# Keys and queries: one store of parts per pair of blocks, replicated when loaded; stores of values and late weights issued by ScalarE's queue

## The chip, the cores and the metric

The kernel runs on one core of a Trainium2 chip. The metric is the device time of one execution in microseconds (us); the slowest core counts, and here there is only one. The engines are called as the profile calls them: PE (matrix multiply, with PEld for its weight loads), DVE, ACT, POOL, and SP, which only issues transfers (DMAs). A transfer is issued by the queue of SP or of ACT, and 16 DMA engines move its bytes.

## The reference, cut to what matters

The input `x` is four images of 64 x 64 pixels with 256 channels, float32. Layer 0 is full self-attention over the 4,096 pixels of each image:

```
q, k, v = x@Wq + bq, x@Wk + bk, x@Wv + bv        # q and k have 32 channels, v has 256
x = gamma * softmax(q @ k^T) @ v + x
```

Layer 1 works on the result: a 3x3 depthwise convolution (three outputs per channel), two 1x1 convolutions with a GELU between them and a residual, then attention over the 3x3 neighbourhood of each pixel, and a second residual. The change touches layer 0 alone: how q, k and v get from where they are computed to where attention reads them.

## The kernel before, in words

Everything is in channels-first layout. An image is cut into 8 blocks of 512 pixels (`NB`). A **slot** is one block of queries: 4 images x 8 blocks = 32 slots. In each slot the kernel goes through the 8 groups `G` of 512 keys of its image, so one group is: four energy matmuls (`energy`, L334, tile `e`), two exponentials on ACT (`weight`, L342, tile `p`), and eight products with the values (`product`, L353, tile `acc`), one half of the exponentials at a time. Energies of group G+1 are issued ahead of the products of group G. `e` has one buffer, so the energies of a group wait until both exponentials of the group before have read it. `p` has three buffers, `ka` (keys of a group) and `v` (values of a group) have three each, `qa` (queries of a slot) has two.

To get q*k in float32 accuracy from a faster matmul format, each of q and k is split into a high part `st` (rounded) and a low part `sl` (what is missing). `project_qk(s)` computes q and k of the two blocks s and s+1 at once (one PSUM tile of 128 rows: q of s, k of s, q of s+1, k of s+1, 32 rows each), ACT writes the high part (L251) and an unrounded copy (L252), DVE subtracts (L253). `st` and `sl` have one buffer each, so the next pair waits for every transfer that reads this one. A key tile `ka` then holds 4 x 32 rows: high, high, low, low; a query tile `qa` holds high, low, high, low. One 128-row matmul thus sums all four products of parts.

Before the change this replication is made on the way out: for each pair of blocks SP issues sixteen 64 KB stores to DRAM (L268 for keys to `packed_k`, L274 for queries to `packed_q`), each of 32 rows, and a group's keys come back in one 256 KB load of 128 rows (`load_keys`, L284), a slot's queries likewise (`spread_queries`, L321). The exception is the first pair: the first queries and the first group's keys go straight from `st`/`sl` into `qa`/`ka`, four copies on SP (L262) and four on ACT (L259).

`project_v` computes 256 pixels of values; ACT copies them out of PSUM (L309) and SP stores them to `packed_v` (L310). For the first image they also stay in `v`; all other values are loaded from `packed_v` (`load_values`, L288).

The order on each engine is the order of the program text (`manual_schedule`). Ahead of slot 0 stand: blocks 0 and 1 fetched, `project_qk(0)`, values of blocks 0 and 1, `project_qk(2)`, `load_keys(0, 1)`, the energies of group 0, the values of block 2. In slot 0, after the second half of group 0, stand `early(4)` (fetch of blocks 4 and 5 from DRAM, L234, tile `xc`, then `project_qk(4)`) and half of the values of block 3; after that of group 1 the other half and `early(6)`; after those of groups 2 to 5 the values of blocks 4 to 7. In the middle of slot 0 (`point == NG`, group 4) SP loads the weights of layer 1 (L80 through `loaded`, and L1228), between the two exponentials of group 5. In the last slot of each image but the last (7, 15, 23), the projections of the next image stand between the groups. Layer 1 starts with slots 2 and 3, at a lag.

Waits are on semaphores. The framework gives the completion of each transfer to one of eight semaphores in turn, across both queues, and a transfer also waits for the one that had its semaphore before it, if nothing later has waited for that.

Of the kernel before, what the change touches and what calls it, by code (L numbers as in the profile page):

```python
# [9 lines left out]
F32 = mybir.dt.float32  # L10
# [6 lines left out]
P = 128  # L17
B, H, W, C = 4, 64, 64, 256
N = H * W
CQK = C // 8  # L20
CH = C // P
HP, WP = H + 2, W + 2
NB = 512
# [15 lines left out]
GRP = P // CQK  # L39
# [3 lines left out]
NSLOT = B * NBLK  # L43
# [10 lines left out]
def attention_then_perception_kernel(  # L54
# [19 lines left out]
    nc = tc.nc  # L74
# [3 lines left out]
    def loaded(src, name, shape=None, queue=None):  # L78
        t = const.tile(list(shape or src.shape), F32, tag=name, name=name)
        (queue or nc.sync).dma_start(out=t, in_=src)  # L80
        return t
# [10 lines left out]
    def unshifted():  # L92
# [6 lines left out]
        def tile_of(shape, tag, name, bufs=1):  # L99
            return pool.tile(shape, F32, tag=tag, name=name, bufs=bufs)  # L100
# [37 lines left out]
        for r in range(4):  # L138
            nc.scalar.dma_start(
                out=bqk2[r * CQK : (r + 1) * CQK, :], in_=b_qk[:, r % 2 : r % 2 + 1]  # L140
# [17 lines left out]
        for r in range(KR):  # L158
            m = near[r * KW : (r + 1) * KW]
            for half in range(2):  # L160

                for sign in (1, -1):
                    nc.gpsimd.affine_select(
                        out=m[:, half], in_=m[:, half], compare_op=ALU.is_ge, fill=0.0,
# [13 lines left out]
        for q in range(0, P, SQ):  # L178
            part = fold[q : q + SQ].rearrange("p (j r) -> p j r", r=SQ)
            nc.gpsimd.affine_select(  # L180
                out=part, in_=part, compare_op=ALU.not_equal, fill=1.0,
# [18 lines left out]
        queries, keys, values, staged = {}, {}, {}, {}  # L200

        packed_q, packed_k = (tc.dram_tile([P, B * N], F32, name=n) for n in ("packed_q", "packed_k"))
        packed_v = tc.dram_tile([P, NSLOT * TPB * C], F32, name="packed_v")
        Q_PARTS, K_PARTS = (0, 1, 0, 1), (0, 0, 1, 1)

        def rows_of(j):
            return slice(j * CQK, (j + 1) * CQK)

        def fetch(s):

# [27 lines left out]
        def project_qk(s):  # L240

            ps = bank("m", f"qk_{s}")
            for kin in range(CH):
                for r in range(2):
                    nc.tensor.matmul(
                        ps[2 * r * CQK : 2 * (r + 1) * CQK, :],
                        lhsT=wqk[:, kin].rearrange("p s d -> p (s d)"),
                        rhs=staged[s + r][:, kin, :], start=(kin == 0), stop=(kin == CH - 1),
                    )
            high, low = (tile_of([P, NB], tag, f"{tag}_{s}") for tag in ("st", "sl"))  # L250
            nc.scalar.activation(high.bitcast(F32R), ps, AF.Identity, bias=bqk2)  # L251
            nc.scalar.activation(low, ps, AF.Identity, bias=bqk2)  # L252
            nc.vector.tensor_tensor(low, low, high, ALU.subtract)  # L253
            parts = (high, low)
            if s == 0:
                queries[0] = tile_of([P, NB], "qa", "qa_0", 2)
                keys[0, 0] = tile_of([P, NB], "ka", "ka_0_0", 3)
                for j in range(GRP):
                    nc.scalar.dma_start(  # L259
                        out=keys[0, 0][rows_of(j), :], in_=parts[K_PARTS[j]][CQK : 2 * CQK, :]  # L260
                    )
                    nc.sync.dma_start(  # L262
                        out=queries[0][rows_of(j), :], in_=parts[Q_PARTS[j]][:CQK, :]
                    )
            for r in range(2):
                at = 2 * r * CQK
                for j in range(GRP):
                    nc.sync.dma_start(  # L268
                        out=packed_k[rows_of(j), bass.ts(s + r, NB)],
                        in_=parts[K_PARTS[j]][at + CQK : at + 2 * CQK, :],  # L270
                    )
                if s + r:
                    for j in range(GRP):
                        nc.sync.dma_start(  # L274
                            out=packed_q[rows_of(j), bass.ts(s + r, NB)],
                            in_=parts[Q_PARTS[j]][at : at + CQK, :],
                        )

        def block(s, G):
            return s - s % NBLK + G  # L280

        def load_keys(s, G):
            keys[s, G] = tile_of([P, NB], "ka", f"ka_{s}_{G}", 3)
            nc.sync.dma_start(out=keys[s, G], in_=packed_k[:, bass.ts(block(s, G), NB)])  # L284

        def load_values(s, G):
            values[s, G] = tile_of([P, TPB, C], "v", f"v_{s}_{G}", 3)
# [5 lines left out]
        def project_v(s, pair, tag="m"):  # L293
            xc = staged[s]
            if s >= NBLK:
                v = tile_of([P, 2, C], "vs", f"vs_{s}_{pair}", 2)
            else:
                if pair == 0:
                    values[0, s] = tile_of([P, TPB, C], "v", f"v_0_{s}", 3)
                v = values[0, s][:, 2 * pair : 2 * pair + 2, :]  # L300
            ps = bank(tag, f"v_{s}_{pair}")
            for i in range(2):
                for kin in range(CH):
                    nc.tensor.matmul(  # L304
                        ps[:, i * C : (i + 1) * C],
                        lhsT=xc[:, kin, bass.ts(2 * pair + i, P)], rhs=wv[:, kin, :],
                        start=(kin == 0), stop=(kin == CH - 1),
                    )
            nc.scalar.copy(v, ps.rearrange("p (t c) -> p t c", c=C))  # L309
            nc.sync.dma_start(  # L310
                out=packed_v[:, bass.ts(2 * s + pair, 2 * C)], in_=v.rearrange("p t c -> p (t c)")
            )

# [4 lines left out]
        def spread_queries(s):  # L318

            queries[s] = tile_of([P, NB], "qa", f"qa_{s}", 2)  # L320
            nc.sync.dma_start(out=queries[s], in_=packed_q[:, bass.ts(s, NB)])  # L321


        energies, weights, sums, accs, lsums, lrdens = {}, {}, {}, {}, {}, {}
# [772 lines left out]
        for i in range(2):  # L1097
            project_v(1, i)
        project_qk(2)
        load_keys(0, 1)  # L1100
        energy(0, 0)
        weight(0, 0, 0)
        weight(0, 0, 1)
# [6 lines left out]
        wlv = pool.tile([P, CH, C], F32, tag="wlv", name="wlv")  # L1110
# [11 lines left out]
        for slot in range(NSLOT):  # L1122
# [3 lines left out]
            k, a = slot - LAG_HID, slot - LAG_ATT  # L1126
# [50 lines left out]
            for point in range(points):  # L1177
                G, half = divmod(point, 2)
                after = slot + (G + 1) // NG, (G + 1) % NG
                if half == 0:  # L1180
                    ahead = slot + (G + 2) // NG, (G + 2) % NG
                    if ahead[0] < NSLOT:
                        load_keys(*ahead)
                    if 0 < ahead[0] < NSLOT:
                        load_values(*ahead)
                    if G == NG // 2 and slot + 1 < NSLOT:
                        spread_queries(slot + 1)
                    if after[0] < NSLOT:
                        energy(*after)
                if after[0] < NSLOT:  # L1190
                    weight(*after, half)
                for do in jobs[point]:
                    do()
                product(slot, G, half)

                if point == 0:
                    add_up(slot, 0, 0)
                if point < points - 1:
                    add_up(slot, *divmod(point + 1, 2))
                else:  # L1200
                    partial_sums(slot)


                if slot < NSLOT - 1:
                    to = sum(share[: point + 1])
                else:
                    to = min(n_steps, -(-(point + 1) * n_steps // (points - 2)))
                    if point < 3:
                        to = min(to, n_mixed // MULT)
                while stepped < to:  # L1210
                    next(conv, None)
                    stepped += 1
                if slot == 0 and point == NG:

                    next(combine)
                    blqk = loaded(b_lqk, "blqk")
                    wperc = loaded(w_perc, "wperc")
                    bperc = loaded(b_perc, "bperc")
                    wup1 = loaded(w_up1, "wup1")
                    bup1 = loaded(b_up1, "bup1")  # L1220
                    wup2 = loaded(w_up2, "wup2")
                    mix_weights(
                        *blocks_of(wup1, MULT, C), *(wmix[:, i] for i in range(4))
                    )
                    y = blocks_of(wup2, CH, P)
                    mix_weights(*y, wmix2[:, 0], wmix2[:, 1], y[1], wmix2[:, 2])
                    bup2 = loaded(b_up2, "bup2")
                    nc.sync.dma_start(out=wlv, in_=w_qkv[:, :, 2 * C :])  # L1228
                    blv = loaded(b_lv.partition_broadcast(P), "blv", [P, C])
                if nxt and half == 1:  # L1230
                    for do in nxt[G]:
                        do()
                    if slot and G + 2 < NBLK:
                        fetch(slot + 1 + G + 2)
# [470 lines left out]
```

## Time and profile before

| what | value |
|---|---|
| time, median of 3 runs | 3399.32 us (3399.2 to 3399.37) |
| the profiled execution | 3399.62 us, its span 3397.9 us |
| PE busy | 3367.3 us (99% of the span) |
| DVE, ACT, POOL busy | 2746.6, 1071.8, 347.5 us |
| DMA | 293.33 MB, mean 86 GB/s |
| loads of keys (L284) | 255 of 256 KB, median 4.0 us to landing |
| loads of values (L288) | 248 of 512 KB, median 3.7 us |
| stores of keys and queries (L268, L274) | 252 of 64 KB, median 1.7 us |
| stores of values (L310) | 64 of 256 KB, median 2.0 and 2.2 us |

The span is the time between the first and the last instruction of the profiled execution; 1.7 us lie around it. A row of the profile's instruction groups gives an engine's busy time for one line of the code, the mean length of one instruction, and the idle time before it with what ended it. The chain of waits goes back from the last instruction to what released each step. The table of windows gives, for a stretch of time, the busy time of each engine, the clock that PE was granted (1.00 is full), the share of time in which the 16 DMA engines were busy (1.00 is all of them), and the rate of all transfers. A transfer's line has the time that its queue took to issue it; when it has landed stands in the list of transfers.

### The profile page before, as it was taken

The numbers are of one execution on the slowest core, as the hardware profiler recorded it, in microseconds if no ns is written. First come the engines' busy times: TensorE is split into PE (matmuls) and PEld (weight loads), VectorE is DVE, ScalarE is ACT, GpSimd is POOL, SyncE is SP. The second block draws the span as 40 slices with busy tenths as digits, with TensorE's granted clock in tenths as the row PEclk, the third lists the DMA queues.
The fourth block names the chain that finished last, engine by engine and source line by source line (L and its number), as shares of the span: only waits on it lengthen the run. The fifth ranks groups of instructions, "written<-read, shape, count | busy, mean of one in ns | idle before, by whom it ended". The sixth has DMA issues, their size and how long they took to land.

```text
span 3397.9 us, 32797 instructions
## 1 busy us (share of the span) xinstructions
PE 3367.3 (99%) x11678; PEld 2117.9 (62%) x11678; DVE 2746.6 (81%) x4455; ACT 1071.8 (32%) x1344; POOL 347.5 (10%) x541
## 2 busy tenths in 40 slices
PE   8999999999999999999999999999999999999999
PEld 4556666666666666666666666666666666666655
DVE  1388888877889888876888898887688888988895
ACT  2233333333333333332333323333233333233331
POOL 1100011100111100110011111001110111110031
PEclk8999999999999999999999999999999999999999
DMA  5432222353222222235222222223522222222200
GB/s 153 137 103 69 75 69 77 94 160 100 78 66 86 86 65 81 72 103 151 94 81 78 66 82 89 65 81 112 161 74 73 81 77 67 82 89 65 70 13 26
DMA packets 178091, 293.33 MB, mean 86 GB/s; under 512 B 75008, under 2 KB 76288, under 8 KB 177792
## 3 DMA queue, kind: packets, MB, share of 16 engines
q1 hardware_dynamic: 177248, 290.56, 27.6%
q8 instruction: 95, 1.56, 0.2%
q10 hardware_dynamic: 672, 0.59, 0.1%
q14 instruction: 76, 0.62, 0.1%
HBM read 240.49 MB, written 50.07 MB: 86 GB/s over the span
## 4 chain that ended last, share of the span: by engine, by line
PE 92%; DVE 6%; SPq 1%; DMA 1%; issue 0%; ACT 0%; ACTq 0%; POOL 0%; DVEq 0%; POOLq 0%
PE acc L353 48%; PE e L334 7%; PE hid_de L611 5%; PE hid_gf L611 5%; PE hid_bc L611 5%; PE lv L924 3%; DVE perc L506 3%; PE lo L1058 3%; PE v L304 3%; PE hid_a L611 2%; PE s L965 2%; PE dx_cd L563 1%; PE dx_ab L563 1%; PE dx_eg L563 1%; DVE den L367 1%; PE g_cd L563 1%
## 5 line engine op out<-in xcount | busy, mean ns | idle before, releaser
L353 PE MATMUL acc<-p,v 128*128 128x512 f32 x4096 | 1833.4, 593 | 0.5 <-DVE o L418 0.5
L353 PEld LDWEIGHTS acc<-p,v 128*128 128x128 f32 x4096 | 770.4, 190 | 794.7 <-issue 775.4
L506 DVE SCALAR_TENSOR_TENSOR perc<-xp,wperc,perc 128x512 f32<-128x512 f32 (+2 forms) x1554 | 1107.4, 774 | 27.4 <-ACT perc L502 27.3
L342 ACT ACTIVATE p<-e 128x1024 f32<-128x1024 f32 x512 | 523.9, 1024 | 1673.6 <-PE e L334 745.9
L367 DVE TENSOR_TENSOR den<-den,p 128x1024 f32<-128x1024 f32 x480 | 585.9, 1221 | 67.9 <-ACT p L342 66.2
L334 PE MATMUL e<-qa,ka 128*128 128x512 f32 x1024 | 365.0, 478 | 11.0 <-DMA ka<-packed_k 11.0
L990 POOL TENSOR_TENSOR lp<-lp,near 128x396 f32<-128x396 f32 x60 | 89.7, 1494 | 2426.1 <-ACT lp L985 2426.1
L334 PEld LDWEIGHTS e<-qa,ka 128*128 128x128 f32 x1024 | 190.4, 190 | 141.2 <-issue 107.7
L611 PE MATMUL hid_de<-perc,wmix 128*128 128x256 f32 x720 | 165.2, 379 | 0.0
L611 PEld LDWEIGHTS hid_de<-perc,wmix 128*128 128x128 f32 x720 | 136.8, 190 | 43.7 <-issue 21.5
L512 DVE TENSOR_TENSOR perc<-perc 128x256 f32<-128x256 f32 x360 | 150.4, 432 | 8.2
L634 ACT ACTIVATE hid<-hid,bup 128x512 f32<-128x512 f32 x120 | 80.1, 714 | 219.7 <-DVE hid L618 219.7
L502 ACT ACTIVATE perc<-xp,bperc,wperc 128x512 f32<-128x512 f32 x192 | 145.3, 805 | 1.7 <-DVE xp L424 1.7
L1013 POOL TENSOR_TENSOR lsum<-lsum,lp 128x99 f32<-128x99 f32 (+1 forms) x179 | 123.1, 694 | 11.7
L924 PE MATMUL lv<-wlv,h 128*128 128x256 f32 x520 | 122.4, 379 | 0.0
L304 PE MATMUL v<-wv,xc 128*128 128x256 f32 x512 | 116.6, 380 | 1.5 <-ACT sl L252 1.4
L1058 PEld LDWEIGHTS lo<-lp,lv 128*128 128x128 f32 x732 | 104.9, 191 | 17.5 <-issue 9.8
L304 PEld LDWEIGHTS v<-wv,xc 128*128 128x128 f32 x512 | 96.9, 190 | 29.3 <-issue 15.0
L924 PEld LDWEIGHTS lv<-wlv,h 128*128 128x128 f32 x520 | 98.7, 190 | 15.5 <-issue 2.2
L1058 PE MATMUL lo<-lp,lv 128*128 128x99 f32 (+1 forms) x732 | 104.7, 291 | 0.0
L342 ACT ACT_TABLE_LOAD x60 | 77.0, 1283 | 82.0 <-PE e L334 81.9
L618 DVE TENSOR_TENSOR hid<-hid_bc,hid 128x512 f32<-128x512 f32 x60 | 41.5, 691 | 73.5 <-PE hid_bc L611 73.5
(198 smaller groups left out, 3125.6 us busy)
## 6 DMA issues: line engine op xcount, KB each, us to landing
v<-packed_v SPq DMA_DIRECT2D x248, 512.0 KB, 3.7
ka<-packed_k SPq DMA_DIRECT2D x255, 256.0 KB, 4.0
xp<-in_x SPq DMA_DIRECT2D x30, 528.0 KB, 4.6
xc<-in_x SPq DMA_DIRECT2D x56, 256.0 KB, 3.9
out<-lo SPq DMA_DIRECT2D x56, 256.0 KB, 2.0
packed_v<-vs SPq DMA_DIRECT2D x48, 256.0 KB, 2.0
qa<-packed_q SPq DMA_DIRECT2D x31, 256.0 KB, 4.0
packed_v<-v SPq DMA_DIRECT2D x16, 256.0 KB, 2.2
```

What stands on the lines that cost most here:

```text
L304: nc.tensor.matmul(ps[:, i * C : (i + 1) * C], lhsT=xc[:, kin, bass.ts(2 * pair + i, P)], rhs=wv[:, kin, :], start=(kin == 0), stop=(kin = ...
L334: nc.tensor.matmul(e[:, j, :], lhsT=key[:, bass.ts(j, P)].bitcast(F32R), rhs=queries[s].bitcast(F32R), start=True, stop=True,)
L342: nc.scalar.activation(p, energies[s, G][:, 2 * half : 2 * half + 2, :], AF.Exp)
L353: nc.tensor.matmul(accs[s][c], lhsT=v[:, 2 * half + i, bass.ts(c, P)], rhs=p[:, i, :], start=(first and i == 0), stop=(G == NG - 1 and hal ...
L367: nc.vector.tensor_tensor(den, den, p, ALU.add)
L502: nc.scalar.activation(acc, win, AF.Identity, bias=bperc[:, half, j : j + 1], scale=wt)
L506: nc.vector.scalar_tensor_tensor(acc, win, wt, acc, ALU.mult, ALU.add)
L512: nc.vector.tensor_tensor(t[:, to, :], t[:, a, :], t[:, b, :], op)
L563: nc.tensor.matmul(ps[:, n * C : (n + 1) * C], lhsT=w(j), rhs=values(j), start=(j == 0), stop=(j == kin - 1),)
L611: nc.tensor.matmul(ps[:, n * C : (n + 1) * C], lhsT=w(j), rhs=mixes[s, j][:, kind, :], start=(j == 0), stop=(j == MULT - 1),)
L924: nc.tensor.matmul(ps[:, half * C : (half + 1) * C], lhsT=keys_of(s, t, half, kin), rhs=wlv[:, kin, :], start=(kin == 0), stop=(kin == CH ...
L1058: nc.tensor.matmul(pv[:, rows, columns(half)], lhsT=lvs[block, t, half][:, bass.ts(c, P)], rhs=near_ws[block, half][:, t, of, :], start=(i ...
```

## The change

- `packed_q` and `packed_k` are replaced by one array `packed`, which holds, for each pair of blocks, high and low parts of q and k once each. `st` and `sl` become one tile `both` (still one buffer), and SP issues one 512 KB store per pair (L269 of the kernel after).
- `load_parts` (its transfers are at L212) makes the replication on loading, in two transfers of 64 rows each. For keys, each transfer reads 32 rows twice (`to_broadcast([2, ...])`); for queries, each reads the high and the low rows. `load_keys` and `spread_queries` use it.
- For the first pair, the queries and the keys of groups 0 and 1 are copied straight from the tile (twelve copies, all on SP, L268), and `load_keys(0, 1)` is gone.
- The stores of values (L304) and the late weights of layer 1 are issued by ACT's queue instead of SP's.

```diff
-        packed_q, packed_k = (tc.dram_tile([P, B * N], F32, name=n) for n in ("packed_q", "packed_k"))
+        packed = tc.dram_tile([NSLOT // 2, 2, 2, 2, CQK, NB], F32, name="packed")
...
+        def load_parts(to, s, which):
+            pair, r = divmod(s, 2)
+            part = packed[pair, :, r, which]
+            for i in range(2):
+                of = part[i : i + 1].to_broadcast([2, CQK, NB]) if which else part
+                nc.sync.dma_start(out=to[2 * i * CQK : 2 * (i + 1) * CQK, :], in_=of)
...
-            high, low = (tile_of([P, NB], tag, f"{tag}_{s}") for tag in ("st", "sl"))
+            both = tile_of([P, 2, NB], "st", f"st_{s}")
+            high, low = both[:, 0, :], both[:, 1, :]
...
             if s == 0:
                 queries[0] = tile_of([P, NB], "qa", "qa_0", 2)
...
-            for r in range(2):
-                at = 2 * r * CQK
-                for j in range(GRP):
-                    nc.sync.dma_start(
-                        out=packed_k[rows_of(j), bass.ts(s + r, NB)],
...
+                for G in range(2):
+                    keys[0, G] = tile_of([P, NB], "ka", f"ka_0_{G}", 3)
+                for part, G in ((0, 0), (1, 0), (0, 1), (1, 1)):
+                    for i in range(2):
+                        for to, at, from_ in (
+                            (queries[0], 2 * i + part, 0), (keys[0, G], 2 * part + i, 2 * G + 1)
+                        )[G:]:
+                            rows, of = (slice(j * CQK, (j + 1) * CQK) for j in (at, from_))
+                            nc.sync.dma_start(out=to[rows, :], in_=both[of, part, :])
+            nc.sync.dma_start(
+                out=packed[s // 2].rearrange("a r q d n -> (r q d) a n"), in_=both
+            )
...
-            nc.sync.dma_start(out=keys[s, G], in_=packed_k[:, bass.ts(block(s, G), NB)])
+            load_parts(keys[s, G], block(s, G), 1)
...
             nc.scalar.copy(v, ps.rearrange("p (t c) -> p t c", c=C))
-            nc.sync.dma_start(
+            nc.scalar.dma_start(
...
-            nc.sync.dma_start(out=queries[s], in_=packed_q[:, bass.ts(s, NB)])
+            load_parts(queries[s], s, 0)
...
         project_qk(2)
-        load_keys(0, 1)
         energy(0, 0)
...
-                    wup1 = loaded(w_up1, "wup1")
+                    wup1 = loaded(w_up1, "wup1", queue=nc.scalar)
...
-                    nc.sync.dma_start(out=wlv, in_=w_qkv[:, :, 2 * C :])
-                    blv = loaded(b_lv.partition_broadcast(P), "blv", [P, C])
+                    nc.scalar.dma_start(out=wlv, in_=w_qkv[:, :, 2 * C :])
+                    blv = loaded(b_lv.partition_broadcast(P), "blv", [P, C], queue=nc.scalar)
```

## The prediction

> **What bounds the kernel now.** First the engines' busy time and the totals of waits, to see whose time is the kernel's.
>
> ```profile
> PE 3367.3 (99%) x11678; PEld 2117.9 (62%) x11678; DVE 2746.6 (81%) x4455; ACT 1071.8 (32%) x1344; POOL 347.5 (10%) x541
> ```
>
> PE is idle for 3397.9 - 3367.3 = 30.6 us. Its own waits name what the change is about:
>
> ```profile
> PE e L334 <- DMA ka<-packed_k: 11.0, 4, 8.4
> PE qk L245 <- DMA xc<-in_x: 5.1, 2, 4.7
> ```
>
> (Total us, times, longest.) Both long waits are in slot 0, as the chain of waits for the first 160 us shows (start, length, what):
>
> ```profile
> 28.17 0.43 SPq L274
> 28.59 0.04 issue
> 28.64 3.16 DMA ka<-packed_k
> 31.80 0.14 issue
> 31.93 2.05 PE e L334 x4
> ...
> 57.36 4.73 DMA xc<-in_x
> 62.09 0.04 issue
> 62.13 3.67 PE qk L245 x6
> 65.81 1.45 PE e L334 x4
> ...
> 77.58 0.92 PE e L334 x4
> ...
> 100.06 0.92 PE e L334 x4
> ```
>
> The first `ka` load stands behind sixteen stores on SP (22.19 to 28.59); the second `xc` fetch stands behind sixteen more and a store of values that waits for ACT. The last three e rows are the energies of groups 3, 4 and 6 of slot 0, 11.24 us apart per group. From 65.81 the chain is PE without a gap to the end of slot 0. The windows view adds the clock (us, then PE, PEld, DVE, ACT, POOL busy, clock, DMA share, GB/s):
>
> ```profile
> 60.00:80.00 20.00, 19.62 (x52) 9.55 (x52) 4.63 (x5) 5.51 (x7) 0.00 (x0) 0.84 0.47 116
> 190.00:252.00 62.00, 62.00 (x181) 32.15 (x180) 60.01 (x90) 19.56 (x21) 3.89 (x5) 1.00 0.31 98
> ```
>
> In slot 2 (second row) PE never waits: what happens to PE in slot 0 reaches the end, unless a transfer comes late.
>
> **What the Trainium skill says.** "DMA: Bandwidth & Descriptors", section "Why a DMA increments its semaphore by 16 and not by 1": a transfer from SP or ACT runs on the largest k up to 16 that divides the outermost dimension (not 1) of both its source and its destination, on the lowest-numbered k engines. In the trace of before the single packets are recorded: 16,736 packets of 4 bytes = 16 x 1,046 transfers, so all ran on 16; none had a small outermost dimension. The new loads have one. In the built program a key load's source is 2 x 32 x 512 (the 2 with stride 0), a query load's 2 x 32 x 512; the destination has 64 rows. So **k = 2**: engines 0 and 1 carry all keys and queries. No run so far shows it. Same page, "Queues, rings and completion order": on each engine one queue's descriptors are consumed in order, and queues alternate; the trace agrees, `v` (3.7 us to land) and the `ka` issued 0.4 us after it (4.0) finish one behind the other. "TensorE: Matmul & The Clock Gate", Part 1: after an idle window PE restarts at half clock; the 0.84 after the wait at 57 to 62 agrees.
>
> **The price of a load on two engines.** 256 KB are 128 packets of 2,048 bytes, 64 on each engine. Packet records: median 84 ns, so 64 x 84 = 5.4 us; 0.7 on 16 engines. The window of slot 2 gives 98/(0.31 x 16) = 19.8 GB/s for an engine, so 6.6 us; the page's Specifications give 27 GiB/s, so 4.5. I take 5.4, the record of just this packet in the quiet slot 2; ends 4.5 and 6.6. The first packet starts 2.4 us after issue (a load of slot 1 issued at 136.6); I take 0.6 from the last one to landing.
>
> **Startup, edit by edit.** Twelve copies on SP from 10.33 at 0.5 each (rows of L262: 0.43 to 0.6) end at 16.4. ACT no longer issues copies (four, 0.7 each), but four stores of values (0.45 to 0.55); before the second `st` it has time for that. One 512 KB store follows; from 64 KB in 1.7 and 256 KB in 2.2 us I get 2.8, landing at 19.2. `st` of pair 1, which waits for it, starts at 19.2 (before 20.18). Two ACT passes (1.27) and two exponentials (1.94) later, 22.5, the energies of group 1 can start: keys lie ready. Gain 31.93 - 22.5 = 9.4.
>
> PE then has 2.05 + 7.82 and wants `xc` of block 4 at 32.4. SP: store of pair 1 at 21.3, landed 24.1, two key issues (0.45 each) to 25.0. Engines 0 and 1 carry them from 26.5 to 31.9; the four `xc` transfers' shares stand behind, to 34.5, landed 35. The projection ends at 36 instead of 34.3. With 1.93 of values, energies of group 2 at 37.9 (45.59). Then 0.93 + 6.87 + 1.74: second `xc` wanted at 47.5. Store at 38.4, keys on engines 0 and 1 41.4 to 46.8, `xc` landed 49.8, projection ends 50.4. **Energies of group 3: 50.5 against 65.81, gain 15.3.** The 1.5 us by which SP waited for values is gone in it.
>
> **The wait that comes.** Store of pair 3 at 52.6. From 55.8 engines 0 and 1 have without pause: keys of groups 4, 5, 6, queries of slot 1 (4 x 5.4 = 21.5), two further loads (1.6), keys of group 7 and of the next slot's group 0 (10.8); and from ACT's queue four stores of values (8 packets each, 2.7), `wup1` (8 x 0.467 = 3.7) and `wup2` (1.3). Sum 41.6: done at 97.4, landed 98.0. ACT needs this: in the built program its nine late weights wait, by the eight semaphores in turn, for earlier transfers; `wlv` for the second half of the next slot's first keys. They stand between the exponentials of group 5. So `wlv` issues at 98.0, `blv` at 98.5, the exponential runs 99.0 to 100.0, and energies of group 6, behind it, start at 101 with queueing. PE's own work would have been ready at 50.5 + 3 x 11.24 = 84.2. **Group 6: 101 against 100.06, +0.9: the gain is used up.** PE idled 16 us and restarts cold: +2.7 (after the wait at 62 before: 3.67 for six of eight projections that take 1.94 in all, and 1.45 for energies of 0.92).
>
> **Slots 1 and 2.** A group is 7.8 us of PE. Engines 0 and 1: keys 5.4, values 1.75 (the window's 0.31 x 7.8 = 2.42 us less 0.67 for keys), queries 5.4/8: 7.8. Just saturated; keys have 15 us from issue to use, so they slip through with +2 (bounds 0 and 5). From slot 3 on a group takes over 10 us.
>
> **Costed at nothing.** 48 later stores of values on ACT (0.45 each): ACT sits idle 3.5 us before such an exponential (679.7 us in 194 waits for products); without that cover, +21.6. Extra SP issues (285 second halves): SP mostly waits. DMA bytes on the way out halve: nothing waits for them later.
>
> **Sum**, against the profiled 3399.62 (0.3 above the median): 0.9 + 2.7 + 2 = +5.6, so **3405**, at the slow edge of no change. A measurement here tells 0.2% (6.8 us) from nothing. The ends of the two-engine price: at 4.5 (70 ns a packet) the 384 packets of keys and queries before group 6 take 5.4 less, the two `xc` waits 1.8, slots 1 and 2 lose nothing: 3396; at 6.6 (103 ns) +7.3 + 2.4 + 13: 3428, which is rival 2 at its worst. With 2 us for startup either way the main case's own range is 3396 to 3412.
>
> **Rivals.**
> (1) Transfers run on 16 engines all the same. For: no trace shows k = 2. Then `xc` and keys are never late: group 3 at 47.7: from 22.5 on PE's own 9.9 + 1.94 + 1.93 + 0.93 + 6.87 + 1.74 + 1.94. Late weights on ACT cost 9 x 0.45 = 4 us plus one key landing, within the 10 us that ACT has between the two groups' energies. -18.1: **3381**, chance 0.17.
> (2) Slower: **engines 0 and 1 saturate.** Over 84 ns per packet, keys, values and queries exceed 7.8 us per group. At 95 ns (mean of all 2,048-byte packets, crowded moments included): 384 packets, +4.2; two `xc` waits +1.4; slots 1 and 2: 8.6 per group, 0.8 x 16 = 12.8 less 7 of lead, in place of 2, +4. **3415**, chance 0.31. Against: slot 2's packets had 84.
> (3) ACT's stores are not covered: 3405 + 21.6 = **3427**, chance 0.07.
> The main case has 0.45.
>
> **Numbers.** Faster: rival 1 and a little of the main case, 0.18. Within 0.2%: most of the main case's lower half and middle, 0.36. Slower: its upper part and rivals 2 and 3, 0.46. Range 3384 to 3418: it leaves out most of rival 1 and rival 3.
>
> **What would show it.** Right: key loads landing at 7 to 9 us instead of 4.0; energies of group 1 near 22.5, of group 3 near 50, of group 6 near 101; a PE wait of about 16 us for ACT between groups 5 and 6; ACT stopped before `wlv`. Wrong: key loads landing in about 4 us (rival 1, and the whole two-engine chain falls), waits of PE for `ka` or `v` in slots 1 and 2 (rival 2), or exponentials late in slots 7, 15, 23 (rival 3).

## The result, and the profile after

The changed kernel takes 3413.88 us (median of 5 runs, 3413.22 to 3416.23) against 3399.2 for the kernel before on the same chip: **ratio 1.0045, interval 1.0031 to 1.006, slower by 14.7 us.** The profiled execution has a span of 3412.2 us (before 3397.9), so 14.3 us are to be found in the traces. The forecast was 3405; the time lies inside its range.

Busy times first (page of the kernel after), then PE's waits (total us, times, longest) and two of ACT's.

```profile
PE 3367.9 (99%) x11678; PEld 2117.8 (62%) x11678; DVE 2748.3 (81%) x4455; ACT 1072.1 (31%) x1344; POOL 347.9 (10%) x541
```

```profile
PE e L328 <- ACT p L336: 14.4, 1, 14.4
PE qk L248 <- DMA xc<-in_x: 8.6, 4, 5.5
PE e L328 <- DMA ka<-packed: 3.7, 6, 1.0
```

```profile
ACT p L336 <- DMA wup<-in_w_up: 17.8, 1, 17.8
ACT p L336 <- DMA ka<-packed: 5.3, 1, 5.3
```

PE's busy time is the same (3367.9 us, before 3367.3); its idle time has gone from 30.6 to 44.3 us. The wait for `ka` (11.0 before, 8.4 at the longest) has nearly gone, the wait for `xc` has grown from 5.1 to 8.6, and one wait of 14.4 us for an exponential is new. ACT itself stands still for 17.8 us ahead of that exponential, and earlier for 5.3 us, when one of its stores of values waits for the semaphore of a key load. The view books the 17.8 under `wup`; the chain, which goes through every issue, leads on to a key load. This chain of waits shows where (start, length, what; compare 31.93, 57.36, 65.81 and 100.06 before):

```profile
28.16 0.64 SPq L212
28.80 0.05 issue
28.84 0.54 SPq L212
...
29.90 3.67 SPq L237
33.56 0.04 issue
33.61 6.62 DMA xc<-in_x
40.23 0.04 issue
40.27 2.99 PE qk L248 x6
43.26 1.93 PE v L298 x8
45.19 0.95 PE e L328 x4
...
49.78 5.51 SPq L237
55.28 0.04 issue
55.33 4.53 DMA xc<-in_x
...
90.39 16.71 DMA ka<-packed
107.09 0.02 issue
107.12 0.62 ACTq L1221
...
107.78 0.60 ACTq L80
...
108.48 1.03 ACT p L336
...
109.56 2.07 PE e L328 x4
111.63 8.17 PE acc L347 x16
```

Read it in three steps. First, behind the two key issues (L212) SP is held for 3.67 us in the issue of one `xc` part, so that the next part is issued only at 33.61 and lands at 40.23; the energies of group 2 start at 45.19 (45.59 before). Second, the next fetch is held for 5.51 us and lands at 59.86, where before it landed at 62.09. Third, the second half of the next slot's first keys, issued at 90.39, lands 16.7 us later; ACT issues `wlv` (L1221) and `blv` (L80) only then, the exponential of group 5 follows, and the energies of group 6 start at **109.56 instead of 100.06: +9.5**. PE restarts cold (2.07 and 8.17 where the same rows take 0.92 and 6.87), and by the end of slot 1 the lag is 12.0: the energies at the turn to slot 2 stand at 203.23 (191.25 before). From there to the last rows of the chain it grows by 1.0 to 13.0, most of it in slot 7 and at the turn to slot 8. The last store to the output lands 12.9 us later than before (3409.07 against 3396.16, by its semaphore), so it adds nothing; 1.3 us more lie between that landing and the end of the span, where only the closing semaphores stand. Together that is 14.3. Run 1 below has the same 1.3 at its end.

That the loads run on two engines is in the packet records. The list of transfers has 570 loads of keys and queries and 435 other transfers on SP's queue. SP's queue shows 8,484 packets of 4 bytes, of which 384 are data of `gam` and `gbv`. 8,484 - 384 = 435 x 16 + 570 x 2, exactly, if each transfer has one such packet for every engine that it runs on. Between 66 and 98 us there are never fewer than two packets in flight, and for 68% of that time exactly two. The prediction's first sign can be read from the semaphores: from the first issue until both halves have landed, a tile of keys takes a median of 9.0 us over 254 tiles, the upper end of the 7 to 9 that it named; between 63.5 and 90 us these loads take 8.8 to 17.8.

### The profile page after: what moved, and what is told of

Same layout as the page of the kernel before. It is cut to its first block, busy times and chain, and to the rows that moved or that the text cites. A ratio compares the mean times of both kernels' runs of the same rounds, so it can differ in the third digit from the quotient of the medians.

```text
span 3412.2 us, 32824 instructions
## 1 busy us (share of the span) xinstructions
PE 3367.9 (99%) x11678; PEld 2117.8 (62%) x11678; DVE 2748.3 (81%) x4455; ACT 1072.1 (31%) x1344; POOL 347.9 (10%) x541
## 4 chain that ended last, share of the span: by engine, by line
PE 88%; DVE 7%; DMA 3%; SPq 1%; issue 0%; ACT 0%; ACTq 0%; DVEq 0%; POOL 0%
PE acc L347 46%; PE e L328 7%; PE hid_bc L605 5%; PE hid_de L605 4%; PE hid_gf L605 4%; PE lv L918 3%; DVE perc L500 3%; PE lo L1052 3%; PE hid_a L605 2%; DMA ka<-packed 2%; PE v L298 2%; PE s L959 2%; PE dx_cd L557 1%; PE dx_ab L557 1%; PE dx_eg L557 1%; DVE den L361 1%
## 5 line engine op out<-in xcount | busy, mean ns | idle before, releaser
L328 PE MATMUL e<-qa,ka 128*128 128x512 f32 x1024 | 363.7, 477 | 18.4 <-ACT p L336 14.4
L1007 POOL TENSOR_TENSOR lsum<-lsum,lp 128x99 f32<-128x99 f32 (+1 forms) x179 | 124.1, 700 | 11.7
```

The source lines that it names most:

```text
L328: nc.tensor.matmul(e[:, j, :], lhsT=key[:, bass.ts(j, P)].bitcast(F32R), rhs=queries[s].bitcast(F32R), start=True, stop=True,)
L1007: nc.gpsimd.tensor_tensor(to, to, near_ws[block, half][:, t_, of, :], ALU.add)
```

## The experiments

**Theory A:** the two-engine loads are the cause of it all: they hold `xc` in the startup, and through a semaphore given in turn they hold ACT. **Theory B:** the cause is which engine issues; nine late weights and the stores of values on ACT stand between its exponentials, whatever the loads. Each result is a median of the runs that were compared; the kernel before had 3398.4 to 3398.7 beside them.

**1. The same loads, in the same number, on 16 engines.**

```diff
-                nc.sync.dma_start(out=to[2 * i * CQK : 2 * (i + 1) * CQK, :], in_=of)
+                nc.sync.dma_start(
+                    out=to[2 * i * CQK : 2 * (i + 1) * CQK, :], in_=of.rearrange("a d n -> d a n")
+                )
...
-                            rows, of = (slice(j * CQK, (j + 1) * CQK) for j in (at, from_))
+                            half, j = divmod(at, 2)
+                            rows = slice(2 * half * CQK + j, 2 * (half + 1) * CQK, 2)
+                            of = slice(from_ * CQK, (from_ + 1) * CQK)
```

> The changed kernel with the rows of a key or query load taken in another order (of each half, row 2d and 2d+1 in place of d and 32+d), so that the outermost dimension of the source is 32 and not 2: as many loads, as many bytes, as many packets, but 16 engines. The twelve direct copies write every second row. Theory A (two engines are the cause of all of it: the xc fetches held behind key loads, and ACT held before wlv by a key load that has not landed): energies of group 1 at 22.8, group 2 near 36, group 3 near 49, group 6 near 85 (34.25 later as before, plus some for the nine late weights on ACT); no PE wait over 4 us; time 3384 to 3390. Theory B (which engine issues is the cause: nine late weights and the stores on ACT stand between exponentials, each waiting for its semaphore, whatever the loads): the wait of PE for the exponential of group 5 stays at 10 us or more, time 3400 to 3412.

Measured: **3381.56 us**, ratio to the kernel before 0.9951 (0.9937 to 0.9965). The chain of this kernel, groups 3 to 6 of slot 0:

```profile
50.75 1.12 PE e L332 x4
51.88 6.87 PE acc L351 x16
58.74 3.45 PE v L302 x16
62.20 0.92 PE e L332 x4
...
84.67 0.92 PE e L332 x4
```

The time is 2.4 us below A's range. Group 3 starts at 50.75 and group 6 at 84.67, with nothing but PE between; the wait for ACT is gone although all nine late weights are still on ACT. SP's queue now shows 16,464 packets of 4 bytes, which is 384 + 16 x 1,005: every transfer ran on 16 engines. A row of SP's issues, of the kernel after, of this one and of the kernel before (start, time to issue, line, transfer), shows the queue itself:

```profile
29.43 8.60 SPq L237 DMA_DIRECT2D xc<-in_x  x4
```

```profile
29.14 3.80 SPq L239 DMA_DIRECT2D xc<-in_x  x4
```

```profile
31.75 6.39 SPq L234 DMA_DIRECT2D xc<-in_x  x4
```

The same four issues take 8.60 us behind two-engine loads and 3.80 behind 16-engine loads. The third row warns against putting every such hold down to two engines: in the kernel before, where all transfers run on 16, the four issues took 6.39 us behind sixteen stores and a key load (4.46 of it in a single issue). Theory A stands, by 32 us; B falls as the main cause.

**2. Four loads of 32 rows in the original order of rows.** The outermost dimension is again 32; it tells the number of engines from the order of the rows.

```diff
-            for i in range(2):
-                of = part[i : i + 1].to_broadcast([2, CQK, NB]) if which else part
-                nc.sync.dma_start(out=to[2 * i * CQK : 2 * (i + 1) * CQK, :], in_=of)
+            for i in range(4):
+                of = part[i // 2 if which else i % 2]
+                nc.sync.dma_start(out=to[i * CQK : (i + 1) * CQK, :], in_=of)
```

> The changed kernel with each block of keys or queries loaded by four loads of 32 rows in the original order of rows; the outermost dimension of each source is 32, so 16 engines, and twice as many issues on SP. Theory A (the number of engines is what counts, not the order of the rows): as the version with 16 engines (3381.56), plus two more issues of 0.6 us ahead of each xc in the startup: 3381 to 3386. Rival (it was the order of rows, or that the two copies of a row are read one after the other): 3395 to 3414.

Measured: 3380.47 us, ratio 0.9947 (0.9933 to 0.9961). The order of rows plays no part, and twice as many issues of loads cost nothing that can be told.

**3. The kernel before, with its key loads alone on two engines.**

```diff
-            nc.sync.dma_start(out=keys[s, G], in_=packed_k[:, bass.ts(block(s, G), NB)])
+            for i in range(2):
+                of = packed_k[2 * i * CQK : (2 * i + 1) * CQK, bass.ts(block(s, G), NB)]
+                nc.sync.dma_start(
+                    out=keys[s, G][2 * i * CQK : 2 * (i + 1) * CQK, :],
+                    in_=of.rearrange("(a d) n -> a d n", a=1).to_broadcast([2, CQK, NB]),
+                )
```

> The kernel before with only its key loads changed: two loads of 64 rows whose source has an outermost dimension of 2 (32 rows, repeated with stride 0), as in the changed kernel; queries, stores, copies, late weights as before. Theory A (the two engines are what costs): a key load lands in some 7 to 9 us instead of 4.0 where it stands alone, so energies of group 1 come about 4 us later than 31.93, group 3 later than 65.81 by 5 to 10, and slots 1 and 2 lose nothing; late weights on SP are held too, but nothing stands behind them on ACT. Time 3404 to 3412. Rival: alone, without the other parts of the change, the key loads are hidden as in the later slots: within 2 us of 3398.4.

Measured: **3482.06 us**, ratio 1.0248 (1.0234 to 1.0262): 83 us, where 6 to 14 were expected. PE's waits in this kernel (its profiled execution took 3476.78, the fastest of five), and two places in its chain, the first in slot 0 and the second in slot 7:

```profile
PE e L339 <- DMA ka<-packed_k: 67.7, 15, 13.8
PE qk L245 <- DMA xc<-in_x: 8.4, 1, 8.4
```

```profile
28.99 0.64 SPq L286
...
29.68 7.83 DMA ka<-packed_k
```

```profile
738.40 0.69 SPq L286
739.08 0.04 issue
739.13 8.52 DMA ka<-packed_k
747.65 0.14 issue
747.78 1.17 PE e L339 x4
```

From the first issue at 28.99 both halves have landed at 37.51, 8.5 us later, close to the price of the prediction (2.4 + 5.4 + 0.6 = 8.4). The expectation was right as far as group 3 of slot 0 (9.1 us later, 5 to 10 expected) and for slots 1 and 2, where no such wait stands. It missed two things. In slot 0 two further waits follow, before groups 4 and 7, so that slot 1 starts 19.7 us late. And in the slots in which the next image is projected (7, 15, 23) sixteen stores precede every second key load on SP and the chain runs SP, load, PE: around these slots the lag grows by 57 us. Of PE's 67.7 us of waits for keys, 22.9 lie in slot 0 and 44.9 around these three. PE's own work, with a restart after each wait, is 16.9 us longer besides, at a mean granted clock of 0.990 (0.997 before). In the changed kernel one store stands in place of the sixteen, and there two-engine loads, those of queries with them, cost 32 us. That the one store covers for the slow loads fits these figures; no run changes it alone.

**4. Late weights back on SP, loads on two engines.**

```diff
-                    wup1 = loaded(w_up1, "wup1", queue=nc.scalar)
+                    wup1 = loaded(w_up1, "wup1")
...
-                    nc.scalar.dma_start(out=wlv, in_=w_qkv[:, :, 2 * C :])
+                    nc.sync.dma_start(out=wlv, in_=w_qkv[:, :, 2 * C :])
```

> The changed kernel with the nine late weights issued by SP again; the values' stores stay with ACT and the loads on two engines. Theory A: the startup is as in the changed kernel (energies of group 3 near 61), ACT is no longer held before the exponential of group 5, so group 6 can start at 61 + 34.25 = 95 to 98; but SP is now held by the same semaphores, and the keys of the groups from 7 on come later. Time 3398 if these keys have enough lead, up to 3412 if PE then waits for them instead. Theory B (issuing on ACT is the whole cost): 3395 to 3399, with no wait of PE for keys after 70 us.

Measured: 3401.89 us, ratio 1.0011 (1.0005 to 1.0018): 12.0 better than the changed kernel. Group 6 starts at 99.63, and the energies at the turn to slot 2 stand at 192.77 (203.23 in the changed kernel): 10.5 us of the gain stand there. The stall of 14.4 us is down to 3.0:

```profile
PE qk L248 <- DMA xc<-in_x: 7.1, 3, 3.3
PE e L328 <- DMA ka<-packed: 4.1, 6, 1.1
PE e L328 <- ACT p L336: 3.0, 1, 3.0
```

The 3.0 left are ACT's again: one of its stores of values waits 4.6 us for the semaphore of a late weight. The startup remains as slow as in the changed kernel (group 3 at 62.10).

**5. Both.** Loads as in 1, late weights as in 4.

> Both: loads on 16 engines, and the nine late weights issued by SP. Theory A: startup as with 16 engines (group 3 near 49), no stall for ACT, group 6 near 83 to 84; time 3382 to 3388, within 3 us of the version with 16 engines alone. Theory B: clearly faster (over 8 us) than the version with 16 engines alone.

Measured: 3381.07 us, ratio 0.9951 (0.9937 to 0.9964). **6. The kernel before, with only the late weights on ACT** (the nine lines of the diff in 4, the other way round).

> The kernel before with only the nine late weights issued by ACT. Theory A: each waits only for transfers that land within some 4 us on 16 engines, and ACT has 10 us between the energies of two groups in slot 0; nothing or a gain of 1 us as SP is freed: 3396 to 3400. Rival (nine issues on ACT hold an exponential whatever the loads): a PE wait of 3 to 8 us for ACT near group 5 or 6, 3402 to 3409.

Measured: 3397.97 us, ratio 0.9999 (0.9991 to 1.0008). Where loads run on 16 engines, it makes no difference that can be told who issues the late weights. The 12.0 us of run 4 arise only from both parts together: a slow load, and an ACT that waits for its semaphore.

**7. Stores of values back on SP, loads on two engines.**

```diff
-            nc.scalar.dma_start(
+            nc.sync.dma_start(
                 out=packed_v[:, bass.ts(2 * s + pair, 2 * C)], in_=v.rearrange("p t c -> p (t c)")
             )
```

> The changed kernel with the values' stores issued by SP again; late weights stay with ACT and the loads on two engines. In the built program wlv then waits for the queries of slot 1 and blv for wup1, in place of keys of the next slot issued later. Theory A: SP also waits for ACT's copies of values again; the stall of PE before group 6 shrinks to some 2 to 8 us, as the load that wlv waits for was issued some 10 us earlier; time 3403 to 3410. Theory B (stores on ACT are the cost): 3395 to 3400. If neither the semaphore nor the stores matter: 3413.

Measured: 3410.51 us, ratio 1.0036 (1.0022 to 1.005), just outside what A expected (3403 to 3410); B is out. PE's wait for ACT is 9.5 us, over the 2 to 8 expected, and it is shorter in part because PE comes later: group 3 starts at 63.68 instead of 61.0, group 6 at 107.43. The chain names the new releaser, a query load (issue, landing, `wlv`):

```profile
88.94 16.03 DMA qa<-packed
...
104.99 0.62 ACTq L1221
```

The semaphore of `wlv` now falls on another load, and the stall follows it. So it is the turn of the semaphore that ties ACT to these loads. By the turn to slot 2 the lag is 11.7 us against 12.0: slot 0 as a whole gains next to nothing from this edit, and the 3.4 us by which the time is shorter come later and are not explained.

**8. The same edit on the version with 16 engines.**

> The version with loads on 16 engines (3381.56), with the values' stores issued by SP as in the kernel before. If the stores of values on SP hold the next xc or keys (in the chain of before, SP waited for ACT's copy of values ahead of the second xc fetch): energies of group 3 come 1 to 4 us after 50.75, time 3382 to 3386. If that wait lies beside others: within 1 us of 3381.6.

Measured: **3391.69 us**, ratio 0.9981 (0.9975 to 0.9988), 10.1 worse than run 1, where 1 to 4 were expected. Its chain:

```profile
47.24 1.74 PE v L302 x8
...
49.00 0.59 ACT v L307
...
49.61 0.34 SPq L308
...
51.22 4.55 DMA xc<-in_x
55.77 0.04 issue
55.81 3.68 PE qk L250 x6
59.49 1.39 PE e L332 x4
```

SP must store these values before it may issue the second `xc`, and the values come from PE itself, just before PE wants `xc`. The fetch cannot run beside PE's work; group 3 is 8.7 us later, with a cold restart in it (3.68 for six projections, where run 1 takes 1.87 for all eight). Some 2 us more come before group 6, where PE waits 1.8 us for an exponential.

**9. The kernel before, with only the values' stores on ACT.**

> The kernel before with only the values' stores issued by ACT. If SP's wait for ACT's copy of values ahead of the second xc fetch sets the second long PE wait of before (57.36): xc lands 1 to 2 us earlier, energies of group 3 at 64 to 65 in place of 65.81, time 3396 to 3398. If ACT's stores hold exponentials instead: 3400 to 3410, with PE waits for ACT in slots 7, 15 and 23.

Measured: 3394.9 us, ratio 0.9989 (0.9982 to 0.9996): 3.7 us, more than expected, and in the place expected: group 3 at 62.05 instead of 65.81.

**10. Loads on 16 engines, keys of group 1 stored and loaded, not copied directly.**

```diff
-                for part, G in ((0, 0), (1, 0), (0, 1), (1, 1)):
+                for part, G in ((0, 0), (1, 0)):
...
         project_qk(2)
+        load_keys(0, 1)
```

> The version with loads on 16 engines (3381.56), with the keys of group 1 not copied directly but stored and loaded as in the kernel before (eight copies in place of twelve, and one load behind the second pair's store). If the direct copy is what the startup gains from: energies of group 1 at 28 to 30 in place of 22.9, xc of the fourth block behind one more load, energies of group 3 at 52 to 55 in place of 50.75, time 3383 to 3387. If PE then waits for xc of the fourth block anyway (group 2 at 39.36 is set by the chain of stores and the fetch, not by group 1): four copies less, 2.4 us earlier, and two issues more, so within 1.5 us of 3381.6 on either side.

Measured: 3381.13 us, ratio 0.9949 (0.9936 to 0.9963), against 3381.56 with the copies. The direct copy of group 1 brings nothing in the time. Its four copies hold SP and the first tile for 2.4 us, and without them the stores, the load and `xc` all come earlier. PE then waits 3.0 us for the load: group 1 starts at 25.63 (24.72 with the copies), group 3 at 51.80 (50.75). That 1 us stays to the end of the work: the last store lands at 3378.36 (3377.18 in run 1). The time does not show it, because only 1.8 us of closing semaphores follow here, and 3.0 in run 1. So the copy is worth about 1 us of the chain, and the ends of the two programs hide it.

**11. `xc` of slot 0 issued by ACT**, with run 4's edit.

```diff
-                    nc.sync.dma_start(out=to, in_=rows[:, c, at, 1 : 1 + W])
+                    (nc.scalar if RING <= s < NBLK else nc.sync).dma_start(
+                        out=to, in_=rows[:, c, at, 1 : 1 + W]
+                    )
```

> The changed kernel with late weights on SP (3401.89), and the eight fetches of xc in slot 0 issued by ACT, so that they do not stand behind the key loads in SP's queue; key loads stay on two engines. If it is the place in the queue behind those loads that makes xc late: xc of the fourth block lands at 31 to 34 in place of 37.4, energies of group 2 at 37 to 40 (44.89), of group 3 at 52 to 57 (62.10), time 3393 to 3398 unless keys come late instead. If engines 0 and 1 themselves are the limit, on whatever queue: xc lands within 2 us of 37.4, and the time is within 2 us of 3402.

Measured: 3405.65 us, ratio 1.002 (1.0012 to 1.0028), 3.8 worse than run 4 and outside both ranges. The first `xc` lands at 39.12, within 2 us of run 4's 37.27. The chain has the second of its four issues on ACT, and the landing of the third, issued at 31.95; the row of all four stands below:

```profile
31.32 0.59 ACTq L237
...
31.95 7.17 DMA xc<-in_x
```

```profile
30.88 5.99 ACTq L237 DMA_DIRECT2D xc<-in_x  x4
```

On a queue without key loads the third part of `xc` still takes 7.2 us from the start of its issue (5.1 in run 1), and 4.1 of them go to the issue itself. So the hold is not one of SP's queue alone; that it comes from what the two engines still have to carry fits this row, and no run separates it further. But ACT's issues stand behind exponentials and start at 30.88, so this run does not say how much the place in SP's queue adds.

**12. A faster version:** run 5 with six of the twelve copies on ACT.

```diff
-                            nc.sync.dma_start(out=to[rows, :], in_=both[of, part, :])
+                            (nc.scalar if i else nc.sync).dma_start(
+                                out=to[rows, :], in_=both[of, part, :]
+                            )
```

> The version with loads on 16 engines and late weights on SP (3381.07), with six of the twelve direct copies issued by ACT. In that version the copies run on SP from 11.2 to 18.2 at 0.6 us each and hold the packed store, and so st of the second pair (PE waits 2.5 us for it) and everything to the first xc. If that chain still sets the start: copies end near 14.8, energies of group 2 come 2.5 to 3.5 us earlier than 38.63, time 3377.5 to 3379.5. If ACT's own work between 10.5 and 22 us then comes late by as much: within 1 us of 3381.

Measured: **3379.4 us**, ratio 0.9943 (0.9929 to 0.9957), the fastest here. Group 2 starts at 37.34 instead of 38.63, 1.3 us and not 2.5 to 3.5 earlier: PE now waits 2.2 us for ACT's copy of values, which stands behind the copies that ACT took over.

## Why the prediction came out as it did

**The mechanism was right.** k = 2 followed from the Trainium skill, "DMA: Bandwidth & Descriptors", section "Why a DMA increments its semaphore by 16 and not by 1", which no run had shown; the packet count above agrees exactly, and run 1, with the same loads on 16 engines, shows that this is what costs. The chain from slow keys over the semaphore of `wlv` and the exponential of group 5 to the energies of group 6 was named in advance and is in the trace row by row. One sentence of the prediction needs a correction: of the 16,736 small packets of before, 384 are data, so there were 1,022 transfers on SP's queue, not 1,046. That all ran on 16 engines stands.

**The number was less right than the mechanism.** The sum gave 5.6 of 14.3 us. The range held the measured time because it was drawn to take in rival 2, whose mechanism did not come about: that is luck.

**The step that failed is the gain of the startup**, "energies of group 3: 50.5 against 65.81". It was 61.0 (the second `xc` landed at 59.86 and two projections followed). Its terms, in order:

- Twelve copies at 0.5, done at 16.4: they take 0.59 plus a gap of 0.05 and are done at 18.2. The first store lands at 21.3 (19.2), and group 1 starts at 24.7 (22.5).
- Store of the second pair, 2.8 us: it took 4.56, landing at 28.1 (24.1). The size was worked out from smaller stores.
- Keys and first `xc`, from the store's landing: 12.1 us (10.9). Nearly right.
- Projections of block 4: 2.99 for six, cold, where 1.0 in all was allowed. The cold restart was charged only once, after the later stall. Group 2 at 45.19, not 37.9.
- Second store to second `xc` landed: 14.5 us (11.4 in the prediction). SP was held in the issue itself. The prediction drew on "Queues, rings and completion order" of the same page for descriptors that stand behind one another on an engine. This trace shows in addition that the issuing sequencer stops: four issues took 8.88 us. The sum had 0.45 for an issue.

**The wait that comes** was sized well: 41.6 us of unbroken work for engines 0 and 1 from 2.4 us after the first issue. That issue came at 63.5, not 53.4; 63.5 + 2.4 + 41.6 + 0.6 = 108.1, measured 107.1. So the +9.5 at group 6, instead of +0.9, is the startup's error of 10.1 at this issue, less 1.5 on the way: it is passed on, since two engines, not PE, set this stretch. The stall itself was 14.4 us (16), the cold restart 2.5 (2.7).

**Slots 1 and 2** were charged +2 and cost nothing. The windows view of the kernel after (us, PE, PEld, DVE, ACT, POOL busy, clock, DMA share, GB/s) shows PE without a pause:

```profile
190.00:252.00 62.00, 62.00 (x180) 31.84 (x179) 52.21 (x77) 19.56 (x21) 4.11 (x6) 1.00 0.32 98
```

The 2,048-byte packets of that window have a median of 84 ns, as assumed (their mean is 91). Rival 2, more than 84 ns a packet with its cost in these slots, gave 3415, close to the measured time, but by a mechanism that did not happen. A matching number is no proof.

**Sum:** 9.5 (group 6) + 2.5 (cold restart) + 0 (slots 1 and 2) + 1.0 (later slots) + 1.3 (the end) = 14.3 instead of 5.6. The last two terms were not in the prediction.

**Rival 1** (16 engines) gave 3381; run 1 measured 3381.56. Its group 3 at 47.7 came at 50.75 by the same copies and stores, made good by 3.5 us that the chain gains between 500 and 3293 us, which the prediction had not counted. They come in steps around slots 7, 15 and 23. At the last two the kernel before has PE waiting for keys (1.0 us before 1592.15 and 1.4 before 2453.59), and run 1 has no such wait; the remaining 1.1 us are not explained. That ACT has room for the late weights where loads are fast is confirmed by runs 5 and 6. **Rival 3** did not come about: no PE wait for ACT of that kind stands in slots 7, 15 or 23.

**"Costed at nothing"** was right for stores of values on ACT as a cost, but they are a gain: 3.7 us alone, 10.1 with 16 engines (runs 9 and 8). What the parts are worth, with 16 engines: stores of values on ACT 10.1 (beside late weights on ACT), direct copy of group 1 about 1 us of the chain and nothing of the time, late weights on ACT nothing that can be told. The single store per pair was not run alone; it is the chief part not tried separately when run 10 (3381.13) is compared with run 9 (3394.9).

## What to carry to other kernels

Look at the outermost dimension of both sides of every transfer before writing it: moving a broadcast of 2 from outermost to second place (`"a d n -> d a n"`) was worth 32 us here, with the same bytes and the same number of transfers. A slow transfer is paid for by whoever has the next turn of its semaphore and whoever stands behind it in the queue, so ask for both before moving issues to an engine that the critical path needs. And take a store of results that have only just been computed out of the queue that must prefetch the next input.

## What the runs showed of the hardware that was not expected

- The issue of a transfer is not a fixed 0.4 to 0.7 us: behind two-engine loads single issues on SP took up to 5.51 us (row 49.78 of the chain after), and with the same loads on 16 engines at most 1.86 us (run 1; 2.6 in runs 5 and 10). The sequencer is held, and with it everything that follows on its queue. In run 11 an issue on ACT was held for 4.1 us, though the slow loads stood on SP's queue; and in the kernel before one issue took 4.46 us with 16 engines throughout.
- Two-engine loads of keys cost 83 us in one program; two-engine loads of keys and queries cost 32 us in another, which has one store where the first has sixteen ahead of every second load on SP.
- A 512 KB store of `st` took 3.02 us to land when issued at 18.24 and 4.56 when issued at 23.54, where the small transfers of `gam` and `gbv` and stores of values ran beside it (3.02 and 4.24 in run 1). These are two points in each trace; what slowed the second was not tried.
